# Sixteen blocks of the FFN's input turned through DRAM and VectorE instead of TensorE, with new places for the E x E stage's sums, softmax halves and look-ups

## The chip, the cores and the metric

One core of one Trainium2 chip runs the whole kernel. The metric is the device time of one execution in microseconds (us). All data is fp32. The engines are named as the profile names them: PE is TensorE (PEld its weight loads), DVE is VectorE, ACT is ScalarE, POOL is GpSimd, SP is SyncE, which issues most DMAs.

## The reference, cut to what matters

x has the shape (2, 2048, 512): 4096 tokens, 512 columns. The attention has no square of tokens: its scores are 512 x 512 (columns by columns, "E x E").

```python
n = layernorm(x)                                   # per token
q, k, v = n @ Wq, n @ Wk, n @ Wv
a = softmax((q^T k) / sqrt(16), axis=-1)           # (2, 512, 512): summed over tokens
x = x + (a v^T)^T @ Wo
g, u, d = lut[gate_idx], lut[up_idx], lut[down_idx]   # 16 values; indices 1376 x 512, 512 x 1376
f = layernorm(x)
x = x + (silu(f @ g^T) * (f @ u^T)) @ d^T
```

## The kernel before, in words

**Blocks and chunks.** 128 tokens are a block; there are 32 (NBLK). Four are a chunk c (NCH is 8), two chunks a pair p (NPR is 4). Every product of matrices is done as a seven-product scheme (Winograd's form of Strassen's), so each operand has extra sums (S1 to S4, T1 to T4), which DVE forms.

**Stages in order of time.**
1. *Gram* (lines 355 to 494): ACT normalizes each block (L175), PE adds up n^T n (L363). The normalized blocks are stored to DRAM (`nd`): those of chunks 3 to 7 as they are made (L361), those of chunks 0 to 2 made a second time by `n_stored` (L458), four each beside chunks 3, 4 and 5. After chunk 5, SP issues the loads of wk and wq, 1 MB each (L336).
2. *E x E* (lines 496 to 634 and 738 to 742): the batch's Gram matrix times the weights, four products for each of two batches: p1, s, t1, m. Each is one call of `square`, which issues seven stages: `a1`, `c1`, the `a4` of the square before, `a2`, `b1`, `c2`, `a3`. A stage is eight PE matmuls (L508); its result is copied by ACT (a1, c1, a2, a4) or added by DVE (b1, c2, a3). The a-stages add up in one PSUM bank, so a2 must wait until ACT has copied a1's result, and a3 for a2's. After each stage come the extra instructions that `beside` lists for it, and `pump(0.7)`. The softmax lies between s and t1: `exp(h)` is a row maximum (DVE, L576), a scaling of it (L577) and two exponentials (ACT, L579); `end(h)` is a reciprocal (DVE, L586) and two scalings (ACT, L588). h is a half of the matrix's rows.
3. *y* (lines 743 to 755): for block k PE forms y = n m (L665). n comes back from `nd` turned: four 64 KB loads a block (`n_load`, L650) and one transpose of 32 x 32 squares on DVE (`n_turned`, L656). `side(k, bank)` then works on earlier blocks: `added(k-1)` adds y to x and starts the second norm, `f_normed(k-6)` normalizes (ACT, L175), `f_turned(k-8)` turns block k-8 for the FFN with four PE transposes (L689) and an ACT copy (L692). `f_summed(p)` forms the FFN's four sums for a pair of chunks. Then `pump(1.0)`.
4. *FFN* (lines 1036 to 1057): 11 tiles f of the 1376 inner columns, for each the four pairs p. A unit `GateUp(f, p)` has the stages a1, c1, (the last unit's) a4, a2, c2, b, a3, eight matmuls each (L769), and after each stage a call of `between()`: 7 slots a unit, 6 in the first. A slot takes the next entry of `todo`, or, when that is empty, calls `pump(0.9)`. `todo` begins with nine entries: what `side` still has to do for blocks 24 to 31, and the last two pairs' sums.
5. *Down* (lines 1064 to 1087): the last product, and the output.

**The order of work** is the program's own on PE, ACT, DVE and SP (`manual_schedule`): nothing overtakes on an engine. PE has 8 PSUM banks.

**The look-ups.** DVE turns 4-bit indices into values by bit tests: `looked_up` (L295) walks a list of 17 jobs: gu0, gu1, wd0 to wd3, gu2, gu3, wd4, gu4, gu5, wd5, gu6 to gu10. Job gu f makes the gate and up weights of FFN tile f: 3 mask pieces, 8 selects (L222), 7 merges (COPY_PREDICATED, L234), then 4 sums. Each piece has a cost in the program's own units: masks 0.74, 0.65 and 0.37, a select 0.75, a merge 1.27, a sum 0.42; a gu job 18.3 and a wd job 16.6 in all. `pump(us)` adds `us` to a budget and issues pieces until it is used up. A gu job waits at a gate until tile f-2 is done (L274). Before tile f starts, whatever is left of job gu f is issued at once:

```python
for f in range(NFT):
    while "S4" not in gu[f]:
        next(lookup)
    ...
    for p in range(NPR):
        ...
        line.run(GateUp(f, p))
    passed[0] = f + 1
```

Of the kernel before, what the change touches and what calls it, by code (L numbers as in the profile page):

```python
# [35 lines left out]
F32 = mybir.dt.float32  # L39
# [10 lines left out]
P = 128  # L50
# [6 lines left out]
def tile_attn_ffn(  # L57
# [13 lines left out]
    nc = tc.nc  # L71
# [33 lines left out]
    wd = wdp.tile([P, NFT, E], F32, tag="wd", name="wd")  # L105
    x1d = dram.tile([NCH, P, J, E], F32, tag="x1d", name="x1d")
    nd = dram.tile([NCH, J, P, E], F32, tag="nd", name="nd")
    hd = dram.tile([NCH, NFT, P, CH], F32, tag="hd", name="hd")


# [2 lines left out]
    def room(tag, name):  # L113
        return keep.tile([P, J, E], F32, tag=tag, name=name)
# [13 lines left out]
    class Norm:  # L128
# [41 lines left out]
            stt(rstd, q, 1.5, r0, ALU.add, ALU.mult)  # L170
            stt(nmr, mean, self.minus, rstd, ALU.mult, ALU.mult)

        def normed(self, j, block, xn=None):
            xn = xn or xnp.tile([P, E], F32, tag="xn", name=f"xn_{self.name}_{j}", bufs=4)
            nc.scalar.activation(  # L175
                xn, block, AF.Identity, bias=self.nmr[:, j : j + 1],
                scale=self.rstd[:, j : j + 1],
            )
            return xn
# [132 lines left out]
    def pump(us):  # L312

        owed[0] = min(owed[0] + us, 2 * us + 1.0)
        while owed[0] > 0:
            cost = next(lookup, None)
            if cost is None:
                return
            owed[0] -= cost
# [140 lines left out]
    for c in range(1, NCH):  # L460
        for j in range(J):
            gram(c, j)
            if STORED <= c < STORED + 3:
                n_stored()
            if c + 1 < NCH and j < 2:
                for i in (2 * j, 2 * j + 1):
                    ln1[c + 1].stats(i, xc[c + 1][:, i, :])
                if j == 1:
                    ln1[c + 1].sqrt(0, J)
            elif c + 1 < NCH and j == 2:  # L470
                pump(0.6)
                ln1[c + 1].rest(0, J)
                pump(0.6)
            elif ahead and c > STORED + 2:
                for op in ahead[:4]:
                    op()
                del ahead[:4]
            else:
                pump(1.9)
            if c == 1 and j == 2:  # L480
                nc.vector.tensor_tensor(
                    lut_x, lut_pairs[:, :, 0], lut_pairs[:, :, 1], ALU.bitwise_xor
                )
            if c == CPB and j == 1:
                gram_out(0)
            if c == CPB + 1 and j == 3:
                wk_sb = load_weight(wk, "a0", "wk_sb")
                wq_sb = load_weight(wq, "a1", "wq_sb")
                wk_ops = right(wk_sb, "wk")
                ahead += wk_ops.todo  # L490
            if c == CPB and j == 3:
                gram_mirror(0)
                g_ops = [left(gs[0], "g_0")]
                ahead += g_ops[0].todo
# [52 lines left out]

    before = [None]

    def square(a, b, dest, name, beside):  # L550

        u = Square(a, b, dest, name)
        last, before[0] = before[0], u
        stages = [u.a1, u.c1, last.a4 if last else lambda: None, u.a2, u.b1, u.c2, u.a3]
        for i, stage in enumerate(stages):
            stage()
            for op in beside.get(i, ()):
                op()  # L560
            pump(0.7)

    class Softmax:

# [32 lines left out]
    assert not ahead  # L597
    square(g[0], wk_ops, p1[0], "p1_0", {
        1: [lambda: gram_mirror(1)], 4: g[1].todo[:2], 5: g[1].todo[2:],
    })  # L600
    square(g[1], wk_ops, p1[1], "p1_1", {
        3: wq_ops.todo[:2], 4: wq_ops.todo[2:], 5: p1_ops[0].todo[:2], 6: p1_ops[0].todo[2:],
    })
    wo_sb = load_weight(wo, "a0", "wo_sb")
    wo_ops = right(wo_sb, "wo")
    att = [room(f"sq{b}", f"a_{b}") for b in range(B)]
# [1 line left out]
    att_ops = [left(att[b], f"att_{b}", ("S1", "S2", "S4")) for b in range(B)]  # L608
    square(wq_ops, p1_ops[0], att[0], "s_0", {
        4: p1_ops[1].todo[:2], 5: p1_ops[1].todo[2:], 6: [lambda: soft[0].exp(1)],  # L610
    })
    square(wq_ops, p1_ops[1], att[1], "s_1", {
        0: [lambda: soft[0].end(1)], 2: [lambda: soft[0].exp(0)], 3: [lambda: soft[0].end(0)],
        4: wo_ops.todo[:2], 5: [*wo_ops.todo[2:], *att_ops[0].todo[:1]],
        6: [*att_ops[0].todo[1:], lambda: soft[1].exp(1)],
    })

    wvT_sb = room("a1", "wvT_sb")
    for k in range(KB):
        for i in range(KB):  # L620
# [1 line left out]
                wvT_sb[:, k, :].rearrange("p (m c) -> p m c", m=KB)[:, :, i * Q : (i + 1) * Q],  # L622
                wvT[k * P : (k + 1) * P, i * P : (i + 1) * P].rearrange("p (m a) -> p m a", a=Q),
            )
    wv_ops = left(wvT_sb, "wv", ("S2", "S1", "S4"))
    t1 = [room(f"a{2 + b}", f"t1_{b}") for b in range(B)]
    t1_ops = [right(t1[b], f"t1_{b}", ("T1", "T2", "T4")) for b in range(B)]
    square(att_ops[0], wo_ops, t1[0], "t1_0", {
        0: [lambda: soft[1].end(1)], 2: [lambda: soft[1].exp(0)], 3: [lambda: soft[1].end(0)],
        5: att_ops[1].todo[:2], 6: att_ops[1].todo[2:],  # L630
    })
    square(att_ops[1], wo_ops, t1[1], "t1_1", {
        4: wv_ops.todo[:2], 5: wv_ops.todo[2:], 6: t1_ops[0].todo,
    })


    nls, nTs, ys, xfs = {}, {}, {}, {}
    xb, xs = {}, {}

    def block(k):  # L640
        return xc[k // J][:, k % J, :]

    def n_load(k):

        if k < NBLK:
            c, j = divmod(k, J)
            nls[k] = sums.tile([P, P // Q, P], F32, tag="e", name=f"nl_{k}")
            rows = nd[c, j].rearrange("(t b) e -> b t e", b=Q)
            for i in range(KB):
                nc.sync.dma_start(nls[k][i * Q : (i + 1) * Q], rows[:, :, i * P : (i + 1) * P])  # L650

    def n_turned(k):

        if k < NBLK:
            nTs[k] = sums.tile([P, KB, P], F32, tag="e", name=f"nT_{k}")
            nc.vector.transpose(  # L656
                nTs[k].rearrange("p m (t b) -> p m t b", b=Q),
                nls[k].rearrange("p t (m a) -> p m t a", a=Q),
            )

    def y_product(k):
        ys[k] = bank(f"y_{k}")
# [6 lines left out]
    def added(k):  # L669
# [6 lines left out]
        if j == J - 1:  # L676
            ln2[c].sqrt(0, J)
            nc.sync.dma_start(x1d[c], xc[c])

    def f_normed(k):  # L680
        xfs[k] = ln2[k // J].normed(k % J, block(k))

    def f_turned(k, bank):
        c, j = k // J, k % J
        if j == 0:
            xb[c] = room(f"x{c - 1}" if c else "a0", f"xb_{c}")
        ps = bank(f"xt_{k}")
        for i in range(KB):
            nc.tensor.transpose(  # L689
                ps[:, i * P : (i + 1) * P], xfs[k][:, i * P : (i + 1) * P], ident  # L690
            )
        nc.scalar.copy(  # L692
            xb[c][:, :, j * P : (j + 1) * P], ps.rearrange("p (k t) -> p k t", k=KB)
        )

    def f_summed(p):

        r = {}

        def half(tag, h):  # L700
            if tag not in r:
                r[tag] = halves.get(tag)
                if r[tag] is None:
                    r[tag] = halves[tag] = room(tag, f"xT_{tag}")
            return r[tag][:, 2 * h : 2 * h + 2, :]

        t1, t2, t4 = (half(*at) for at in SUMS_AT[p])
        b11, b21 = xb[2 * p][:, 0:2, :], xb[2 * p][:, 2:4, :]
        b12, b22 = xb[2 * p + 1][:, 0:2, :], xb[2 * p + 1][:, 2:4, :]
        sub(t1, b12, b11)  # L710
        sub(t2, b22, t1)
        sub(b12, b22, b12)
        sub(t4, b21, t2)
        xs[p] = {"11": b11, "21": b21, "22": b22, "T3": b12, "T1": t1, "T2": t2, "T4": t4}

    halves = {}
    SUMS_AT = [
# [3 lines left out]
        [("sq1", 1), (f"x{NCH - 1}", 0), (f"x{NCH - 1}", 1)],  # L721
    ]

    def side(k, bank):

        if 0 <= k - 8 < NBLK:
            f_turned(k - 8, bank)
        if k - 1 < NBLK:
            added(k - 1)
        if k % J == 1 and 0 <= (k - 5) // J < NCH:  # L730
            ln2[(k - 5) // J].rest(0, J)
        if 0 <= k - 6 < NBLK:
            f_normed(k - 6)
        done = (k - 12) // J
        if k % J == 0 and done in (1, 3):
            f_summed(done // 2)

    m_sb = [room(f"sq{b}", f"m_{b}") for b in range(B)]
    square(wv_ops, t1_ops[0], m_sb[0], "m_0", {4: t1_ops[1].todo[:2], 5: t1_ops[1].todo[2:]})
    square(wv_ops, t1_ops[1], m_sb[1], "m_1", {  # L740
# [2 lines left out]
    for k in range(NBLK):  # L743
        if k:
            n_turned(k + 1)
            n_load(k + 3)
        y_product(k)
        if k == 0:
            before[0].a4()
            n_turned(1)  # L750
            n_load(2)
            n_load(3)
        else:
            side(k, bank)
        pump(1.0)
    pps.release()
    sums.release()
    ffn = tc.alloc_tile_pool(name="ffn", bufs=1, reuse_waits="tile")
# [116 lines left out]
        else:  # L875
            pump(0.9)

    def tr(name):
        return psum("tr", name)

    def drained(k):
        side(k, tr)
        if k == NBLK + 1:
            f_summed(2)

    todo += [lambda k=k: drained(k) for k in range(NBLK, NBLK + 8)]
    todo.append(lambda: f_summed(3))


    wd_ops = []  # L890
# [145 lines left out]
# [3 lines that stand above are left out]
        if f == NFT - 1:  # L1039
# [8 lines left out]
            h = Hidden(0)  # L1048
            todo += by_two(down_sums(hps["dT"]))
        for p in range(NPR):  # L1050
            if f == NFT - 1 and p == 1:
                h.rest_of()
                todo += by_two(h.sums())
            if f == NFT - 1 and p == 3:
                units = [Down(h, 0)]
            line.run(GateUp(f, p))
# [82 lines left out]
```

## Time and profile before

| | |
|---|---|
| median of 3 runs | 1118.92 us (1118.81 to 1119.29) |
| the profiled execution | 1118.62 us, span 1116.6 us |
| first matmul, end of the last | 7.1 us, 1112.5 us |
| PE transposes of the FFN's input (L689) | 128, four for each of 32 blocks |
| DVE transposes (L656) | 32, 702 ns each |
| the L175 ACT pass of one block | 803 to 805 ns |
| copy of a turned block (L692) | 586 ns |
| merge (L234), select (L222) | 1304 ns, 804 ns |
| 128x512 add or subtract on DVE | 680 to 692 ns |

Stages by the timeline: Gram's matmuls to 81.6 us, E x E to 185.5, y to 307.3, FFN to 842, Down to 1112.5. The profile's page gives busy shares, the span in 40 slices, the chain of work that ended last, and groups of instructions; "idle before" is the time an engine stood still ahead of an instruction, with what released it. Instructions on DVE and ACT overlap their neighbours a little, so that two in a row start closer together than one lasts.

### The profile page before, as it was taken

How to read it: one execution, taken by the hardware profiler on the slowest of the kernel's cores; microseconds unless marked ns; L12 is line 12 of the kernel's file. 1: busy time of each engine (PE TensorE's matmuls, PEld its weight loads, DVE VectorE, ACT ScalarE, POOL GpSimd, SP SyncE). 2: the span in 40 equal slices, each digit the busy share in tenths (PEclk: the TensorE clock that was granted, in tenths of full speed). 3: DMA queues.
4: the chain of work that ended last, by engine and by line, in shares of the span. 5: the costliest groups of instructions: out<-in, count | busy, mean ns of one | idle time of the engine just before them, and what ended most of it. 6: DMA issues, size and time to landing. Idle time of an engine off the chain costs nothing.

```text
span 1116.6 us, 10381 instructions
## 1 busy us (share of the span) xinstructions
PE 1095.0 (98%) x3580; PEld 659.6 (59%) x3580; DVE 684.1 (61%) x1251; ACT 310.9 (28%) x583; POOL 14.7 (1%) x31
## 2 busy tenths in 40 slices
PE   7999899999999999999999999999999999999998
PEld 4668677444454444444444444444437888888887
DVE  6877887677766757788777575855553344333341
ACT  4642332456562222222322222222221000000000
POOL 0000000000000000000000000000000000000000
PEclk9999999999999999999999999999999999999999
DMA  8460302444211111111111111111415443345421
GB/s 337 173 226 21 74 19 76 157 137 140 94 57 66 56 48 66 57 54 55 68 62 51 57 38 69 40 38 49 144 47 179 156 160 121 107 164 167 159 66 38
DMA packets 72180, 108.76 MB, mean 97 GB/s; under 512 B 15152, under 2 KB 31536, under 8 KB 70208
## 3 DMA queue, kind: packets, MB, share of 16 engines
q1 hardware_dynamic: 69936, 100.70, 26.7%
q0 software_dynamic: 2192, 7.41, 2.2%
q8 instruction: 28, 0.46, 0.2%
q14 instruction: 24, 0.20, 0.1%
HBM read 60.37 MB, written 47.71 MB: 97 GB/s over the span
## 4 chain that ended last, share of the span: by engine, by line
PE 94%; DVE 3%; ACT 1%; DMA 1%; issue 0%; SPq 0%; DVEq 0%; ACTq 0%
PE a_g L769 27%; PE a_d L769 14%; PE c_g L769 14%; PE y L665 10%; PE c_d L769 7%; PE b_g L769 7%; PE gp L363 5%; PE b_d L769 4%; PE xt L689 1%; PE ea_p L508 1%; PE ea_m L508 1%; DMA nd<-xn_a 1%; PE ea_t L508 1%; PE ec_m L508 1%; PE ec_p L508 1%; ACT a L579 0%
## 5 line engine op out<-in xcount | busy, mean ns | idle before, releaser
L125 DVE TENSOR_TENSOR c<-c_g,u 128x512 f32<-128x512 f32 (+1 forms) x44 | 30.4, 690 | 146.2 <-PE c_g L769 139.4
L665 PE MATMUL y<-m,nT 128*128 128x512 f32 x256 | 114.0, 592 | 0.0
L769 PE MATMUL c_g<-xb,w 128*128 128x512 f32 (+1 forms) x176 | 82.8, 593 | 0.8 <-DVE w L122 0.8
L769 PE MATMUL a_g<-xb,s 128*128 128x512 f32 (+1 forms) x176 | 82.8, 592 | 0.8 <-DVE c L125 0.8
L769 PE MATMUL a_g<-xb,w 128*128 128x512 f32 (+1 forms) x176 | 82.7, 592 | 0.0
L769 PE MATMUL b_g<-xb,w 128*128 128x512 f32 (+1 forms) x176 | 82.7, 592 | 0.0
L769 PE MATMUL a_g<-xT_a,s 128*128 128x512 f32 (+1 forms) x176 | 82.7, 592 | 0.0
L363 PE MATMUL gp<-xn_a 128*128 128x512 f32 (+3 forms) x256 | 72.4, 445 | 8.7 <-ACT xn_a L175 8.7
L665 PEld LDWEIGHTS y<-m,nT 128*128 128x128 f32 x256 | 46.8, 190 | 49.4 <-issue 49.0
L821 ACT ACTIVATE h<-h 128x512 f32<-128x512 f32 (+1 forms) x44 | 27.7, 630 | 161.9 <-DVE h L125 161.9
L363 PEld LDWEIGHTS gp<-xn_a 128*128 128x128 f32 x256 | 45.1, 196 | 35.8 <-issue 16.6
L769 PE MATMUL a_g<-xT_sq,s 128*128 128x512 f32 (+1 forms) x132 | 62.0, 592 | 0.0
L222 DVE TENSOR_SCALAR gu<-idx_gu,lut_x,lut_sb 128x1024 int32<-128x1024 int32 (+1 forms) x77 | 59.1, 792 | 0.0
L769 PEld LDWEIGHTS a_g<-xb,s 128*128 128x128 f32 (+1 forms) x176 | 32.8, 188 | 43.2 <-issue 38.9
L769 PEld LDWEIGHTS c_g<-xb,w 128*128 128x128 f32 (+1 forms) x176 | 32.8, 188 | 42.7 <-issue 41.1
L769 PEld LDWEIGHTS b_g<-xb,w 128*128 128x128 f32 (+1 forms) x176 | 32.9, 188 | 42.0 <-issue 42.0
L769 PEld LDWEIGHTS a_g<-xT_a,s 128*128 128x128 f32 (+1 forms) x176 | 32.9, 188 | 41.5 <-issue 41.5
L769 PEld LDWEIGHTS a_g<-xb,w 128*128 128x128 f32 (+1 forms) x176 | 32.9, 188 | 41.5 <-issue 41.3
L234 DVE COPY_PREDICATED gu<-b_gu,gu 128x1024 f32<-128x1024 int16 (+1 forms) x44 | 56.2, 1278 | 0.7
L769 PE MATMUL a_d<-dT,hs_a 128*128 128x256 f32 x224 | 56.2, 379 | 0.0
L234 DVE COPY_PREDICATED wd<-b_wd,wd 128x1024 f32<-128x1024 int16 (+1 forms) x42 | 50.9, 1213 | 0.5
L125 DVE TENSOR_TENSOR r<-r,a_d 128x256 f32<-128x256 f32 x32 | 13.5, 421 | 54.8 <-PE a_d L769 54.8
(238 smaller groups left out, 1736.6 us busy)
## 6 DMA issues: line engine op xcount, KB each, us to landing
hd<-h SPq DMA_DIRECT2D x80, 256.0 KB, 2.0
h<-hd SPq DMA_DIRECT2D x40, 512.0 KB, 6.7
nl<-nd SPq DMA_DIRECT2D x128, 64.0 KB, 2.0
x1d<-x SPq DMA_DIRECT2D x8, 1024.0 KB, 4.3
r<-x1d SPq DMA_DIRECT2D x32, 256.0 KB, 4.0
out_dram<-r SPq DMA_DIRECT2D x32, 256.0 KB, 2.4
x<-in_x_dram SPq DMA_DIRECT2D x7, 1024.0 KB, 14.1
nd<-xn_a SPq DMA_DIRECT2D x20, 256.0 KB, 2.1
```

Source lines behind the costliest of these rows:

```text
L125: nc.vector.tensor_tensor(dest, a, b, ALU.add)
L222: vec.tensor_scalar(dest.bitcast(I32), idx, lut_x[:rows, k : k + 1], lut_i[:rows, at : at + 1], ALU.bitwise_and, ALU.bitwise_xor,)
L234: vec.copy_predicated(dest, masks[level - 1], t)
L363: nc.tensor.matmul(gp[b][i][:, i * P :], xn[:, i * P : (i + 1) * P], xn[:, i * P :], start=c % CPB == 0 and j == 0, stop=c % CPB == CPB - ...
L508: nc.tensor.matmul(ps[:, m, :], self.a[a][:, k, m * P : (m + 1) * P], self.b[b][:, k, :], start=first and m == k == 0, stop=k == 1, skip_g ...
L665: nc.tensor.matmul(ys[k], nTs[k][:, i, :], m[:, i, :], start=(i == 0), stop=(i == KB - 1))
L689: nc.tensor.transpose(ps[:, i * P : (i + 1) * P], xfs[k][:, i * P : (i + 1) * P], ident)
L769: nc.tensor.matmul(ps, lhsT, rhs, start=first and i == 0, stop=i == len(pairs) - 1, skip_group_check=not first,)
L821: nc.scalar.activation(self.h0, self.h0, AF.Silu)
```

## The change

**Turning.** Blocks 16 to 31 (`EARLY` is 16) are no longer turned by PE. ACT writes their normalized rows with the columns in another order (`quarters`), SP stores them to a new DRAM tensor `xnd`, four 64 KB loads bring each back (`f_load`), and one DVE transpose (`f_turned_late`) puts it in its place. Store and load are 5 blocks apart in the y stage, load and transpose 2. What remains after y is 20 entries of `todo` instead of 9. The FFN's sums become a generator with one sum a step: pairs 0 and 1 over four blocks of y each, pairs 2 and 3 over entries of `todo`.

**E x E.** `square` takes a list of seven pump rates; the softmax halves and the sums of wo, att, wv and t1 are listed at other stages. In y, `pump` gets 1.0 up to block 21 and 0.5 after that.

**Gram.** `n_stored` runs beside chunks 3, 5 and 6 instead of 3, 4 and 5.

```diff
-            if STORED <= c < STORED + 3:
+            if c in (CPB - 1, CPB + 1, CPB + 2):
                 n_stored()
...
-            pump(0.7)
+            pump(rate[i])
...
     square(g[0], wk_ops, p1[0], "p1_0", {
...
-    })
+    }, (1.2, 1.2, 1.2, 1.2, 0.3, 0.3, 1.2))
     square(g[1], wk_ops, p1[1], "p1_1", {
...
-    })
+    }, (1.2, 1.2, 1.2, 0.3, 0.3, 0.3, 0.3))
...
     square(wq_ops, p1_ops[0], att[0], "s_0", {
         4: p1_ops[1].todo[:2], 5: p1_ops[1].todo[2:], 6: [lambda: soft[0].exp(1)],
-    })
+    }, (1.0, 1.0, 1.0, 1.0, 0.3, 0.3, 0.3))
     square(wq_ops, p1_ops[1], att[1], "s_1", {
-        0: [lambda: soft[0].end(1)], 2: [lambda: soft[0].exp(0)], 3: [lambda: soft[0].end(0)],
-        4: wo_ops.todo[:2], 5: [*wo_ops.todo[2:], *att_ops[0].todo[:1]],
-        6: [*att_ops[0].todo[1:], lambda: soft[1].exp(1)],
-    })
+        1: [lambda: soft[0].end(1)], 2: [lambda: soft[0].exp(0)], 3: wo_ops.todo[:2],
+        4: [lambda: soft[0].end(0)], 5: [*wo_ops.todo[2:], *att_ops[0].todo[:2]],
+        6: att_ops[0].todo[2:],
+    }, (0.5, 0.5, 0, 0, 0, 0, 0))
...
     square(att_ops[0], wo_ops, t1[0], "t1_0", {
-        0: [lambda: soft[1].end(1)], 2: [lambda: soft[1].exp(0)], 3: [lambda: soft[1].end(0)],
-        5: att_ops[1].todo[:2], 6: att_ops[1].todo[2:],
-    })
+        1: [lambda: soft[1].exp(1)], 2: [lambda: soft[1].exp(0)], 3: [lambda: soft[1].end(1)],
+        4: [lambda: soft[1].end(0)], 5: att_ops[1].todo[:2], 6: att_ops[1].todo[2:],
+    }, (0, 0, 0.5, 0.5, 0.5, 0, 0))
     square(att_ops[1], wo_ops, t1[1], "t1_1", {
-        4: wv_ops.todo[:2], 5: wv_ops.todo[2:], 6: t1_ops[0].todo,
-    })
+        2: wv_ops.todo[:1], 3: wv_ops.todo[1:2], 4: [*wv_ops.todo[2:3], t1_ops[0].todo[0]],
+        5: [*wv_ops.todo[3:], t1_ops[0].todo[1]], 6: t1_ops[0].todo[2:],
+    }, (1.0, 1.0, 0.7, 0.7, 0, 0, 0))
...
+    EARLY = NBLK // 2
+
     def f_normed(k):
-        xfs[k] = ln2[k // J].normed(k % J, block(k))
+        c, j = divmod(k, J)
+        xfs[k] = ln2[c].normed(j, block(k), quarters=k >= EARLY)
+        if k >= EARLY:
+            nc.sync.dma_start(xnd[c, j], xfs[k])
...
+    def f_load(k):
+        fls[k] = xnp.tile([P, E], F32, tag="xn", name=f"fl_{k}", bufs=4)
+        reload(fls[k], xnd[k // J, k % J])
+
+    def f_turned_late(k):
+        turn(f_place(k), fls[k])
...
-        if 0 <= k - 8 < NBLK:
-            f_turned(k - 8, bank)
+        if 0 <= k - 8 < EARLY:
+            f_turned(k - 8)
...
+        if k - 11 in range(EARLY, NBLK) and k < NBLK:
+            f_load(k - 11)
+        if k - 13 in range(EARLY, NBLK) and k < NBLK:
+            f_turned_late(k - 13)
+        p, i = divmod(k - 16, 2 * J)
+        if 0 <= p < NPR // 2 and i < 4:
+            if i == 0:
+                f_pairs[p] = f_sums(p)
+            next(f_pairs[p])
...
-        pump(1.0)
+        pump(1.0 if k < EARLY + 6 else 0.5)
...
-    todo += [lambda k=k: drained(k) for k in range(NBLK, NBLK + 8)]
-    todo.append(lambda: f_summed(3))
+    for i, what in enumerate([
+        dict(turns=[19], loads=[21]), dict(turns=[20], loads=[22]), dict(loads=[23]),
+        dict(turns=[21]), dict(turns=[22], loads=[24]), dict(turns=[23], loads=[25]),
+        dict(pair=2), dict(pair=2, turns=[24], loads=[26]), dict(pair=2),
+        dict(turns=[25], loads=[27]), dict(pair=2, turns=[26], loads=[28]),
+        dict(turns=[27], loads=[29]), dict(turns=[28], loads=[30]), dict(turns=[29], loads=[31]),
+        dict(turns=[30]), dict(turns=[31]), dict(pair=3), dict(pair=3), dict(pair=3), dict(pair=3),
+    ]):
+        late(i, **what)
```

`late` appends one entry to `todo`: the first eight call `side` as before, then come the listed transposes, loads and one sum of the pair.

## The prediction

> **What bounds the kernel now.** I read the page first. PE is busy for 98% of the span and in every slice:
>
> ```profile
> PE 1095.0 (98%) x3580; PEld 659.6 (59%) x3580; DVE 684.1 (61%) x1251; ACT 310.9 (28%) x583; POOL 14.7 (1%) x31
> ```
>
> The chain of waits gives PE 94%. So the time is PE's work plus PE's waits. An edit counts when it takes work from PE, ends a PE wait, or makes a new one. Second, PE's own waits:
>
> ```profile
> PE gp L363 <- ACT xn_a L175: 8.7, 3, 7.1
> PE ea_t L508 <- ACT t L520: 2.8, 1, 2.8
> PE ec_t L508 <- DVE a L122: 1.6, 1, 1.6
> PE ec_m L508 <- DVE t L122: 1.3, 1, 1.3
> PE c_g L769 <- DVE w L122: 0.8, 1, 0.8
> ...
> PE ea_s L508 <- ACT a L520: 0.4, 1, 0.4
> PE ea_s L508 <- ACT a L529: 0.3, 1, 0.3
> PE ea_t L508 <- ACT t L529: 0.3, 1, 0.3
> ```
>
> Of the 8.7, 7.1 is the start. Six lines lie in E x E; one (`c_g <- w`) is a look-up that came late. Third, the chain by time, for what PE's transposes cost:
>
> ```profile
> 218.24 0.44 PE xt L689 x4
> 218.68 3.43 PE y L665 x8
> 222.12 0.44 PE xt L689 x4
> ```
>
> Four transposes take 0.436 us of PE between two y products of 3.43.
>
> **Transposes off PE.** 16 blocks x 0.436 = **-7.0**, eight blocks in y, eight in the FFN. That is all PE gets back if nothing new makes it wait. What replaces them:
> - DVE, 16 transposes of 0.70. In y (k 29 to 31) a period falls to 3.43; DVE has n_turned 0.62, added 0.70, pump about 0.5, the transpose 0.62, every fourth block 0.96 of norm: 2.4 to 3.4. For k 24 to 27 a sum of 1.15 stands in its place: 3.0, or 3.9 once, under a block (3.43) of lead. Hidden.
> - ACT, 16 copies of 586 ns fewer. The re-ordered write of L175 is not in the trace. Nearest rows: L692's copy into pieces and a plain copy both 586 ns; a DVE transpose 702 against 680 for an add. So 0 to 3% of 803 ns; I take 0. Doubled it would still fit a period in which ACT works 1.8.
> - SP, 16 stores (0.32 to issue, landing in 2.1) and 64 loads (0.43, landing in 2.0). A load stands two blocks (6.9) before its transpose in y. Hidden there.
>
> **E x E.** From the timeline, start to start, a stage takes 1.727. The six late ones lose 0.59, 0.44, 1.76, 2.98, 0.44, 1.44, and each restart 0.1 more: 8.25. The costliest, with its columns start, duration, engine, line, instruction:
>
> ```profile
> 138.08 0.72 ACT L579 ACTIVATE a<-a,nb 128x512 f32<-128x512 f32 x1 [8.61 <-DVE nb L577]
> ...
> 139.50 0.56 ACT L520 COPY t<-ea_t 128x512 f32<-128x512 f32 x1
> ```
>
> The copy that t1_0's a2 needs is queued on ACT behind exponentials that waited for a row maximum. I walked the new order through with these rows' durations (add 0.60, after its own operand 0.72; maximum 1.25; scaling of it 0.2; exponential pair 1.43, scaling pair 1.24, copy 0.56; time stamps as before up to 115):
> - s_0: two look-up sums leave the place ahead of a3's add, which starts at 117.67, not 118.34. Exponentials at 119.84; a1's copy, now ahead of `end(1)`, is done at 121.83, and a2 is due at 121.96: 0.1 left of 0.59.
> - s_1: maximum 124.04, exponentials 125.50, a2's copy done 127.50; a3 is due at 127.25: 0.3 and a restart of 0.1 remain. This wait isn't removed.
> - wo's first sums go ahead of `end(0)`; att's S3 is ready at 130.03, needed at 131.1: 1.76 gone.
> - t1_0: `exp(1)` stands behind c1's copy, so a1's copy (131.9) is early for a2 (134.56): 2.98 gone. Next late is a2's copy behind `exp(0)`: 139.41 against 139.74. It fits by 0.3.
> - t1_1's a1 (141.47) needs `end(0)`, done at 141.90: 0.3 new.
> - t1's T3 is formed at 152.1, needed at 155.3: 1.44 gone.
>
> Left: 0.8 of 8.25, so **-7.4**. Bounds: -5.5 (t1_0's a2 copy and one more miss by a maximum each) and -8.2.
>
> **Gram.** Four L175 passes and stores move from chunk 4 to 6, behind the 2 MB of weights in SP's queue. Chunk 7's passes need the stores of chunk 6, which landed at 71.80, 72.42, 73.05, 73.67; with a store between each pair the spacing is 1.25, and 1.11 is PE's per block: **+0.4** (0 to 1).
>
> **The look-ups: the new wait.** Count the budget in the program's units; it can be counted without a time. Gram's pumps are unchanged and issue 22.9. E x E before: 56 x 0.7 = 39.2; now 32.0. y before: 32; now 22 x 1.0 + 10 x 0.5 = 27. So the FFN starts at 94 before, at 82 now. The slots without pump grow from 9 to 20. Tile 2 starts at slot 55 (6 + 7 x 7). Before, wd3 is done at slot 19, the gate opens at 27, gu2 is done at slot 45, ten ahead. Now 35 slots x 0.9 bring 82.1 to 113.6, but gu2 ends at 3 x 18.3 + 4 x 16.65 = 121.6. In whole pieces what is left is a merge, two selects, three merges and the four sums. The `while` ahead of tile 2 issues them in one go, and PE's next matmul needs the last merge. The trace shows this place once, at tile 4, where two sums were left:
>
> ```profile
> 499.69 1.30 DVE L234 COPY_PREDICATED w<-b_gu,gu 128x1024 f32<-128x1024 int16 x1
> 500.89 0.67 DVE L125 TENSOR_TENSOR h<-b_g,p 128x512 f32<-128x512 f32 x1
> 501.85 0.69 DVE L125 TENSOR_TENSOR c<-a_g,p 128x512 f32<-128x512 f32 x1 [0.29 <-PE a_g L769]
> 502.46 0.68 DVE L827 TENSOR_TENSOR h<-h,c 128x512 f32<-128x512 f32 x1
> 503.06 0.42 DVE L125 TENSOR_TENSOR s<-w 128x256 f32<-128x256 f32 x1
> ```
>
> PE started tile 4 at 501.65. Laid on this pattern, tile 2 has DVE busy with: merge to 500.89, add, select 501.50, add 502.22, product 502.83, select 503.43, then the burst from 504.27: merge 1.21, selects 0.72 and 0.83, merges 1.34, 1.34 (each needs the one before) and 1.31, done at 511.02. That is 9.4 after PE's due start, with the restart **+9.5** (8.5 to 10.5). Nothing covers it: PE is in order and its bank is free.
>
> At tile 4 the same count leaves the last merge for the slot before and all four sums for the burst: merge 500.95, add 502.16, product 502.77, last merge 503.37 to 504.68, so PE waits 3.1 where it waited 0.95: **+2.1** (1.5 to 2.6).
>
> **The clock after 9 us of idling.** The trace has PE starting cold: the first 128x512 matmuls took 1141 ns, later ones 594:
>
> ```profile
> L363 PE MATMUL gp<-xn_a 128*128 128x512 f32 x2 | 2.1, 1141 | 7.1 <-ACT xn_a L175 7.1
> ...
> L363 PE MATMUL gp<-xn_a 128*128 128x512 f32 x25 | 12.9, 594 | 0.0
> ```
>
> (the first line for the window from 7, the second for 13 to 40). The first block lasted 4.43 (7.10 to 11.53), the second 2.49, the third 2.16: the start cost 2.27 + 0.33 = 2.6. Idling of 2.8 at 137 was followed by matmuls of full speed; at the end the granted clock is 1.00 until 1114.7 and then 0.50, 2.2 after the last matmul. Nine us of idling is beyond both, so I take **+2.6** (0, as after 137, to 3.4). The Trainium skill, "TensorE: Matmul & The Clock Gate", Part 1, speaks against the change here: by it an idle window of about 3.4 us halves the clock and as long a busy one restores it, which would be an estimated 1.7 in place of 2.6 and the total 0.9 lower; the start in this trace, 5 us to full speed, is longer than the page's window.
>
> **FFN's first 20 slots.** A slot is now 1.72 instead of 2.15 for the first eight. ACT: a1's copy, the last block's statistics and one L175 pass stand ahead of c1's copy, done 5.2 after the FFN's start; c2 is due at 5.15: +0.2. DVE: 13 transposes (8.1), 8 sums (9.2), 1.7 of norm, and 2.9 units' own work at 3.1 make 28 in 34.3. But SP's loads wait in turn for the 1 MB x1d store, for L175 and for DVE's products, and landings push DVE some 3 us late at slots 4 to 12. Pair 3's third sum is then done at 36.5 and c1 of that unit due at 36.05. **+0.5** together (0 to 1.5).
>
> **Sum.** -7.0 - 7.4 + 0.4 + 9.5 + 2.1 + 2.6 + 0.5 = +0.7 on the profiled execution's 1118.62, which lies 0.3 below the median of the three runs: **1119.3**. No change that a measurement of this kernel can tell, which is about 0.2%, or 2.2 us.
>
> **Rivals.**
> - *The clock stays* and the small terms are nothing: -7.0 - 8.2 + 9.5 + 2.1 = -3.6, so 1115. For it: 2.8 us of idling cost nothing. Against it: the half clock at the end came sooner. 0.15.
> - *The look-ups aren't late*, since the budget runs differently from my count: without 9.5, 2.1 and 2.6 the time would be 1105. Against it: the count puts the job starts of before where the trace has their first mask (gu2 358.9, gu3 406.9, gu4 469.0). 0.02.
> - *Slower: the second trip through DRAM holds DVE* in slots 9 to 20, where a load is followed by its transpose two slots (3.4 us) later. From about 4.5 us per load on, the lateness reaches PE at pair 3. y's loads took up to 8 us (262.06 to 270.04) behind an x1d store, which is what stands ahead here too. Price 3 to 5: 1123. Against it: the median is 2.0. 0.17.
> - *The clock also falls at tile 4*: the idling there is some 2.8, as at 137 where it did not; 2.6 more, 1121.9. 0.08.
>
> The forecast's own case has the remaining 0.58, 1116.8 to 1121.2. Range 1115.3 to 1123.3, which cuts off the tail of the first and third rivals and the second. Faster 0.17, same 0.58, slower 0.25 (the third and fourth rivals).
>
> **What would show it.** PE's waits: one of about 9.4 for a merge (`w`, L234) at the start of tile 2, one of about 3 at tile 4; in E x E one of about 0.3 at s_1's a3, nothing over 1. Matmuls at 514 or so above 1.1 us for some 5 us. y periods of 3.43 from block 24 on. L689 with 64 transposes. I'd be wrong if the burst is shorter, if E x E keeps a wait of over 1 us, or if PE waits in slots 0 to 20 by more than 1.5.

## The result, and the profile after

| | before | after |
|---|---|---|
| median, lowest, highest (us) | 1118.95, 1118.10, 1119.39 (6 runs) | 1124.19, 1121.76, 1127.84 (6 runs) |
| ratio of the times | 1 | 1.0050, 95% interval 1.0031 to 1.0069 |
| profiled execution, its span | 1118.62, 1116.6 | 1127.84, 1125.7 |
| mean granted clock of PE | 0.999 | 0.991 |

The change made the kernel slower by 0.5%, 0.9 us beyond the range's upper end. "No change" was forecast. The profiled execution of after is the slowest of its six. Its parts below add up to +9.2 where the medians differ by +5.2; where those 4 us lie is told under "The step under both", further down.

The code moved down by some lines: the merges are L242 (L234 before), the adds L128 and L125, the turning transposes L661, the FFN's matmuls L808, E x E's L516, the remaining PE transposes L712. The loads of `xnd` are issued at L657, its stores at L701. An FFN stage is four PE instructions in the trace, not eight as written above; a stage of E x E is eight. (One 128x512 product of the program shows there as two PE instructions.)

The page's busy times and its row of the granted clock, after:

```profile
PE 1095.9 (97%) x3516; PEld 656.0 (58%) x3516; DVE 696.3 (62%) x1267; ACT 303.6 (27%) x567; POOL 14.6 (1%) x31
...
PEclk9999999999999989998999999999999999999999
```

PE has 64 instructions fewer, yet it was busy 0.9 longer: some matmuls ran slowly. The clock row shows two slices below 9, the 15th and the 19th (394 to 422 and 507 to 535). PE's own waits, after (sum, times, longest):

```profile
PE a_g L808 <- DVE w L242: 11.8, 2, 9.2
...
PE c_g L808 <- DVE xb L125: 2.3, 1, 2.3
PE a_g L808 <- DVE c L128: 2.1, 2, 1.4
...
PE ea_s L516 <- ACT a L537: 0.3, 1, 0.3
```

Of the six E x E waits of before one of 0.3 is left. Two waits for a merge came (9.2 at tile 2, 2.7 at tile 4), and two more in the FFN's tile 0: 1.4 for an add on DVE (`c`, L128) and 2.3 for one of pair 3's sums (`xb`, L125). The first matmuls of each place tell the rest. PE's timeline, after, with the columns start, duration, what, and idle time before; at full speed a stage starts 1.72 after the one before:

```profile
337.36 3.68 PE L808 MATMUL c_g<-xb,w 128*128 128x512 f32 x4 [2.33 <-DVE xb L125]
340.84 1.92 PE L808 MATMUL a_g<-xb,s 128*128 128x512 f32 x4
...
406.88 3.78 PE L808 MATMUL a_g<-xb,w 128*128 128x512 f32 x4 [9.19 <-DVE w L242]
410.46 2.94 PE L808 MATMUL c_g<-xb,w 128*128 128x512 f32 x4
413.24 1.88 PE L808 MATMUL a_g<-xb,s 128*128 128x512 f32 x4
...
508.76 3.78 PE L808 MATMUL a_g<-xb,w 128*128 128x512 f32 x4 [2.66 <-DVE w L242]
512.33 3.20 PE L808 MATMUL c_g<-xb,w 128*128 128x512 f32 x4
```

After each of the three waits a stage takes about twice its time. It isn't the operands: the same stages elsewhere take 1.72. It is the clock. The windows of after (window, length, busy time of PE, PEld, DVE, ACT, POOL, granted clock, DMA share, GB/s):

```profile
337.50:340.90 3.40, 3.40 (x5) 1.33 (x6) 3.37 (x5) 0.00 (x0) 0.23 (x1) 0.50 0.21 77
402.30:412.60 10.30, 5.72 (x7) 2.52 (x8) 10.09 (x15) 0.59 (x1) 0.71 (x1) 0.50 0.17 51
508.20:515.00 6.80, 6.24 (x8) 2.63 (x9) 6.38 (x12) 0.59 (x1) 0.00 (x0) 0.50 0.10 39
```

The clock was half in all three. Three falls of the clock, then, where the prediction counted on one.

**The account**, in starts of the same instructions, after less before, both profiled executions:

| stretch | measured | forecast |
|---|---|---|
| Gram and E x E, to the first y product | -7.55 | -7.0 (-7.4 + 0.4) |
| y | -3.51 | -3.5 |
| FFN tile 0, without its eight blocks' transposes (-3.49) | +6.56 | +0.5 |
| tile 2's first matmul against tile 1's start (the burst) | +9.36 | +9.5 |
| the rest of tile 2 (the clock) | +2.92 | +2.6 |
| tile 4's wait (2.66 in place of 0.80) and restart | +2.82 less 0.95 | +2.1 |
| the rest of tile 4 (the clock) | +3.1 | 0 |
| sum, transposes of the FFN (-3.49) with it | +9.2 | +0.7 |

So two rows failed: tile 0, and the clock in tile 4. Of tile 0's 6.56, 1.76 is the half clock behind pair 3's wait (that stage took 3.48 from start to start, not 1.72); the rest is waits and their restarts.

### The profile page after: what moved, and what is told of

Read it like the earlier page. It is cut to its first block, busy times and chain, and to the rows that moved or that the text cites. A ratio compares the mean times of both kernels' runs of the same rounds, so it can differ in the third digit from the quotient of the medians.

```text
span 1125.7 us, 10379 instructions
## 1 busy us (share of the span) xinstructions
PE 1095.9 (97%) x3516; PEld 656.0 (58%) x3516; DVE 696.3 (62%) x1267; ACT 303.6 (27%) x567; POOL 14.6 (1%) x31
## 4 chain that ended last, share of the span: by engine, by line
PE 93%; DVE 3%; SPq 1%; ACT 1%; DMA 1%; issue 1%; DVEq 0%; ACTq 0%
PE a_g L808 25%; PE a_d L808 14%; PE c_g L808 13%; PE y L680 10%; PE c_d L808 7%; PE gp L371 6%; PE b_g L808 6%; PE b_d L808 4%; PE ea_t L516 1%; SPq L657 1%; PE ea_p L516 1%; PE ea_m L516 1%; PE ea_s L516 1%; PE xt L712 1%; PE ec_t L516 1%
## 5 line engine op out<-in xcount | busy, mean ns | idle before, releaser
L128 DVE TENSOR_TENSOR c<-c_g,u 128x512 f32<-128x512 f32 (+1 forms) x44 | 30.3, 689 | 145.0 <-PE c_g L808 138.1
L808 PE MATMUL a_g<-xb,w 128*128 128x512 f32 (+1 forms) x176 | 86.5, 615 | 11.8 <-DVE w L242 11.8
L808 PE MATMUL c_g<-xb,w 128*128 128x512 f32 (+1 forms) x176 | 87.0, 619 | 2.3 <-DVE xb L125 2.3
L808 PE MATMUL a_g<-xb,s 128*128 128x512 f32 (+1 forms) x176 | 82.9, 593 | 2.1 <-DVE c L128 2.1
L808 PE MATMUL a_g<-xT_a,s 128*128 128x512 f32 (+1 forms) x176 | 82.8, 593 | 0.1
L808 PE MATMUL b_g<-xb,w 128*128 128x512 f32 (+1 forms) x176 | 82.7, 592 | 0.0
L808 PEld LDWEIGHTS a_g<-xb,w 128*128 128x128 f32 (+1 forms) x176 | 33.8, 194 | 56.2 <-issue 42.7
L808 PEld LDWEIGHTS c_g<-xb,w 128*128 128x128 f32 (+1 forms) x176 | 34.4, 196 | 48.3 <-issue 43.3
L808 PE MATMUL a_g<-xT_sq,s 128*128 128x512 f32 (+1 forms) x132 | 62.0, 592 | 0.0
L808 PEld LDWEIGHTS a_g<-xb,s 128*128 128x128 f32 (+1 forms) x176 | 33.1, 189 | 46.3 <-issue 39.0
L808 PEld LDWEIGHTS a_g<-xT_a,s 128*128 128x128 f32 (+1 forms) x176 | 32.9, 188 | 43.0 <-issue 42.0
L808 PEld LDWEIGHTS b_g<-xb,w 128*128 128x128 f32 (+1 forms) x176 | 33.0, 188 | 42.5 <-issue 42.5
L242 DVE COPY_PREDICATED gu<-b_gu,gu 128x1024 f32<-128x1024 int16 (+1 forms) x44 | 56.4, 1281 | 0.9
L808 PE MATMUL a_d<-dT,hs_a 128*128 128x256 f32 x224 | 56.2, 378 | 0.0
L242 DVE COPY_PREDICATED wd<-b_wd,wd 128x1024 f32<-128x1024 int16 (+1 forms) x42 | 50.9, 1212 | 0.8
L837 ACT COPY p<-a_g 128x512 f32<-128x512 f32 (+1 forms) x44 | 25.7, 584 | 86.0 <-PE a_g L808 86.0
```

The lines of the kernel that those rows point to most:

```text
L128: nc.vector.tensor_tensor(dest, a, b, ALU.add)
L242: vec.copy_predicated(dest, masks[level - 1], t)
L808: nc.tensor.matmul(ps, lhsT, rhs, start=first and i == 0, stop=i == len(pairs) - 1, skip_group_check=not first,)
L837: nc.scalar.copy(self.p1, self.a)
```

## The experiments

Theory A, formed from this account: the burst at tile 2 with its cold restart costs some 12, tile 4 up to 5, SP's issuing of the loads 4 to 5; the E x E edits and the transposes gain what was forecast. Rival theories are in the expectations.

### The look-ups on time

```diff
-            pump(0.9)
+            pump(1.2 if passed[0] < 2 else 1.0 if passed[0] < 4 else 0.9)
```

in `between()`, everything else as after: the budget of tiles 0 to 3 runs faster, so that nothing is left for a burst.

> The changed kernel with larger look-up budgets in the first four FFN tiles (1.2 a slot in tiles 0 and 1, 1.0 in tiles 2 and 3, instead of 0.9), so that by the count no piece is left over at any tile's start. Theory A (the loss is look-ups issued in a burst that PE waits for, and the half clock after it): the wait of 9.2 at tile 2 and of 2.7 at tile 4 disappear from PE's waits, and so do the slow matmuls behind them: 1124.2 - 9.4 - 2.9 - 2.8 - about 1.5 = 1107.6. Rival B (VectorE has no room for these pieces, so they only move the waiting into tiles 0 and 1): PE waits of 5 us or more in all inside tiles 0 and 1, 1118 or above.

Measured: **1107.40** (1106.81 to 1108.54, four runs; before beside it 1118.69), ratio 0.9902 (0.9887 to 0.9916). Theory A's number. The longest of PE's waits behind the start:

```profile
PE c_g L808 <- DVE xb L125: 2.4, 1, 2.4
```

Both waits for merges are gone and none took their place; pair 3's of 2.4 stays, with the slow stage behind it. Against after's +5.2, this is 16.5 us less. Some 1.1 of it is a gain over before: its own late look-up at tile 4 (0.8 and a restart) is on time too. The look-ups that the change displaced out of E x E and y, and what followed from them, are even so more than the whole loss.

### The loads of xnd over two queues

```diff
-    def reload(t, rows):
+    def reload(t, rows, queues=(nc.sync, nc.sync)):
...
-            nc.sync.dma_start(t[i * Q : (i + 1) * Q], rows[:, :, i * P : (i + 1) * P])
+            queues[i % 2].dma_start(t[i * Q : (i + 1) * Q], rows[:, :, i * P : (i + 1) * P])
...
-        reload(fls[k], xnd[k // J, k % J])
+        reload(fls[k], xnd[k // J, k % J], (nc.sync, nc.scalar))
```

> The changed kernel with every second f_load DMA issued by ACT instead of SP. Theory A (pair 3's sums come late because SP needs 1.9 us to issue a block's four loads and works without a pause from 300 to 329): the waits of 1.4 at 322 and 2.3 at 334 go, and the half clock behind the second: 1124.2 - 4.4 - 0.8 = 1119. Rival C (VectorE itself is too full in the first 20 slots): the waits stay, 1124. If ACT's own waits for a free buffer hold up its copies, PE waits for ACT there instead.

Measured: **1119.16** (1116.77 to 1121.56, ten runs), ratio 1.0006 (0.9996 to 1.0016): 4.8 below after's +5.2. Here is why the loads mattered, first SP's own timeline in after (start, busy time, what):

```profile
313.65 7.31 SPq L657 DMA_DIRECT2D fl<-xnd  x12
321.06 0.38 SPq L831 DMA_DIRECT2D hd<-h  x1
321.48 3.77 SPq L657 DMA_DIRECT2D fl<-xnd  x8
```

SP issued so, one behind the other with hardly a pause, from 301.5 to 329.5, as a rule 0.47 from one load to the next, four loads to a block (one issue, at 316.1, took 1.99, for a reason that the trace doesn't show): it was itself the bound, and the loads left it late, one block every 2 us or more. Their landing was not slow: 2.3 from issue, as in the group of DMA issues. DVE paid first: in after it stood 1.20, 1.87 and 1.08 for loads ahead of the last three transposes (326.9 to 331.3), and pair 3's sums come behind these. Its waits for the loads in after, then in this run:

```profile
DVE xb L661 <- DMA fl<-xnd: 14.9, 12, 2.5
```

```profile
DVE xb L661 <- DMA fl<-xnd: 7.2, 6, 2.8
```

and PE last. PE's timeline of this run at the place where after has 2.33 of waiting and a slow stage:

```profile
333.49 1.98 PE L808 MATMUL c_g<-xb,w 128*128 128x512 f32 x4 [0.40 <-DVE xb L125]
```

0.40, and a stage of full speed behind it. Pair 3's third sum was done 37.0 after the FFN's start, where the forecast had 36.5 and after 40.8. The wait of 1.4 at 323 went too, so DVE had room for its own work in these slots. The burst of 9.2 at tile 2 stayed, as it should: the two losses are separate. After tile 4's wait, 2.66 here too, the stage lasted 1.98: this time the clock stayed.

### The idle time filled

After, with nine matmuls of an identity, whose result nothing reads, ahead of tile 2's first product:

```diff
+            if f == 2 and p == 0:
+                idle = fps.tile([P, E], F32, tag="idle", name="idle", bufs=1)
+                for _ in range(9):
+                    nc.tensor.matmul(idle, ident, xs[0]["11"][:, 0, :], start=True, stop=True)
...
             line.run(GateUp(f, p))
```

> The changed kernel with nine 128x512 matmuls on PE ahead of tile 2, into a PSUM bank that nobody reads, which fill 7.7 of the 9.2 us in which PE waits there. Theory A (idling lowers the clock, and the first 5 to 6 us after it run at half speed): the wait shown shrinks to about 1.5, the matmuls behind it last 592 ns, the time falls by 2.9 to 1121.3. Rival D (the half clock is no result of the idling, or costs nothing): 1124 or more.

Measured: **1121.42** (1119.58 to 1123.00, ten runs), ratio 1.0025 (1.0016 to 1.0035): 2.5 below after's +5.2, with useless work added. PE's timeline (the nine products are 18 PE instructions):

```profile
396.94 7.89 PE L1112 MATMUL idle<-xb,ident 128*128 128x512 f32 x18
406.33 1.98 PE L808 MATMUL a_g<-xb,w 128*128 128x512 f32 x4 [1.50 <-DVE w L242]
```

The burst still ends at 406.3, so its 9 us are still lost, but tile 2 begins at full speed. That separates the burst (9.4) from the clock (2.9 in the trace, 2.5 here in medians).

### The E x E order alone, and the turning alone

One kernel is before with nothing but after's E x E section: the lists of `beside`, the seven rates of each `square`, and the order of wv's sums. The other is the version of the next section, but with before's E x E section put back.

> The kernel before with the E x E stage's new order and pump rates alone; turning, Gram, y and FFN as before. By the count its look-ups are as much in time as before (three pieces left at tile 4). Theory A: E x E is 7.6 shorter and nothing is given back: 1118.95 - 7.6 = 1111.4. Rival E (the smaller budgets of the squares are paid later by waits for look-ups): 1116 or above.

Measured: **1111.23** (1110.70 to 1111.43, four runs), ratio 0.9934 (0.9919 to 0.9949): -7.5, where -7.4 was forecast. Two of PE's waits (L508 and L770 are this kernel's lines of the E x E and FFN matmuls); the second is all that E x E has left:

```profile
PE c_g L770 <- DVE w L122: 0.8, 1, 0.8
...
PE ea_s L508 <- ACT a L529: 0.3, 1, 0.3
```

By the count E x E's lower rates delay the look-ups here too, but y's `pump(1.0)` and the nine entries of `todo` were left as they were, and tile 4's old wait of 0.8 didn't grow: the cut in E x E alone makes no look-up late.

> The same with the E x E stage of the kernel before (its order and its 0.7 rates): turning and Gram's moved stores, with both repairs. Theory A: the turning is worth 7.0 less the waits that stay in tile 0 (1.0), and 1.0 at tile 4: 1118.7 - 7.0 = 1111.7, so that the two gains add up to that of both within 0.5. Rival G (the turning's gain is partly taken back by VectorE in the y stage, hidden in the other runs): y periods above 3.43 from block 24 on, 1114 or more.

Measured: **1112.33** (1111.22 to 1112.80, four runs; before beside it 1119.23), ratio 0.9937 (0.9920 to 0.9954): -6.9. The transposes give back what PE spent on them, if nothing new is late. That the sum is so near 7.0 is partly chance: it holds the 1.1 at tile 4, which the faster budget gives, and losses of about the same size. One of these stands in its timeline; first the same place in before, then here:

```profile
140.12 1.99 PE L508 MATMUL ea_t<-T_wo,S_att 128*128 128x256 f32 x8 [2.82 <-ACT t L520]
```

```profile
140.09 3.45 PE L516 MATMUL ea_t<-T_wo,S_att 128*128 128x256 f32 x8 [2.82 <-ACT t L528]
```

This is the wait of 2.8 at 137 that the prediction took as proof that such idling is free. In the profile of before the stage behind it lasted 1.99. Here, behind the same wait of the same instruction, it lasted 3.45. That cost 1.4, of which 0.9 was left where y began.

### Both new waits gone

After, with the edits of the first two experiments together.

> The changed kernel with both repairs: larger look-up budgets in tiles 0 to 3 and every second f_load issued by ACT. Theory A: what is left is the gains, E x E 7.6 and turning 7.0, the 1.0 that tile 4 waited before, less about 1.0 of waits in tile 0: 1118.7 - 14.6 = 1104, with no half clock between start and end. Rival F (the two repairs disturb each other, since tile 1's fuller VectorE and ACT's queue meet): 1106 or more with a new wait above 1 us in tile 0 or 1.

Measured: **1104.12** (1103.39 to 1104.46, four runs; before beside it 1119.23), ratio 0.9866 (0.9852 to 0.9881): 15.1 below before and some 20 below after; the fastest version here. The page's busy times:

```profile
PE 1087.8 (99%) x3516; PEld 653.5 (59%) x3516; DVE 695.1 (63%) x1267; ACT 303.9 (28%) x567; POOL 14.7 (1%) x31
```

PE is busy 8.1 less than in after with the same 3516 instructions. In after's three windows PE was busy for 15.4 at half clock, which at full speed would have been 7.7: nearly all of it. No wait behind the start's is longer than 0.8, pair 3's is 0.2, and the granted clock's row holds 9 in every slice. The parts add up: -7.5 (E x E alone) and -6.9 (turning alone) make -14.4 for -15.1, and the 0.7 between them is of the size of the 0.9 that the slow stage just shown cost, in the turning-alone kernel only. The tile 4 gain of 1.1 is in both -6.9 and -15.1.

### Idling in doses

What decides whether the clock falls? Two kernels, each the version just shown, with a stated number n of in-place multiplications by 1.0 on DVE, which change no value, ahead of seven FFN tiles, so that PE idles there for 1.9 to 5.9 us:

```diff
+            if p == 0:
+                for _ in range({3: 2, 4: 3, 5: 4, 6: 5, 7: 6, 8: 8, 9: 12}.get(f, 0)):
+                    nc.vector.tensor_scalar_mul(gu[f]["11"], gu[f]["11"], 1.0)
...
             line.run(GateUp(f, p))
```

(the other kernel has the numbers 6, 5, 12, 4, 3, 2, 8).

> Both repairs, and at the start of tiles 3 to 9 VectorE multiplies a quarter of the tile's weights by one 2, 3, 4, 5, 6, 8 and 12 times, which holds PE up for idle times of about 2.0, 2.5, 2.9, 3.4, 3.8, 4.7 and 6.5 us. It asks from which idle time the granted clock falls. If a full window of the clock record (its low stretches are multiples of 3.41) has to be idle, it falls never below 3.4, always above 6.8, by chance between. If less suffices, as at 2.3 and 2.7 in the changed kernel, it falls at some of the doses below 3.4 too. Cost of a fall: 1.7 to 3.4.

> As the doses before, in another order (6, 5, 12, 4, 3, 2 and 8 times at tiles 3 to 9): the same idle times meet other moments of the record. If the fall is set by the idle time alone, the same doses fall in both; if by where in a window the idling lies, doses between about 2 and 5 differ from run to run.

One execution each: 1142.83 and 1140.33, of which 24.4 are the seven added waits. What counts is the 14 idle stretches:

| idle (us) | 1.91 | 2.24 | 2.24 | 2.57 | 2.90 | 2.90 | 3.23 | 3.25 | 3.70 | 3.88 twice, 5.00, 5.19, 5.88 |
|---|---|---|---|---|---|---|---|---|---|---|
| clock fell | no | yes | no | yes | yes | no | yes | no | yes | yes |

No threshold of length fits: 2.24 fell and 3.25 didn't. The same wait of 2.24, PE's timeline of the first kernel and then of the second:

```profile
495.97 3.68 PE L808 MATMUL a_g<-xb,w 128*128 128x512 f32 x4 [2.24 <-DVE w L1111]
```

```profile
659.42 1.98 PE L808 MATMUL a_g<-xb,w 128*128 128x512 f32 x4 [2.24 <-DVE w L1111]
```

What fits is the phase. In every trace here the granted clock changes only at instants that lie a multiple of 3.413 us apart. Windows of the first kernel laid on that grid, columns as before; an idle of 2.24 ends at 495.97, one of 3.25 at 549.25:

```profile
492.69:496.10 3.41, 1.17 (x4) 0.32 (x3) 2.32 (x7) 0.63 (x1) 0.00 (x0) 1.00 0.22 84
496.10:499.52 3.42, 3.42 (x5) 1.35 (x6) 3.38 (x7) 0.00 (x0) 0.00 (x0) 0.50 0.14 55
...
547.29:550.70 3.41, 1.45 (x4) 0.73 (x5) 3.31 (x10) 0.00 (x0) 0.00 (x0) 1.00 0.57 216
550.70:554.10 3.40, 3.40 (x10) 1.49 (x9) 2.17 (x4) 1.17 (x2) 0.00 (x0) 1.00 0.00 0
```

The 2.24 lay inside one window: PE worked 1.17 of it, was idle for 66%, and the next window ran at 0.50. The 3.25 was cut by an edge: PE worked 1.45 of the fuller one, was idle for 57%, and the clock stayed. Over all traces here the clock fell each time that one window was idle for over 58%, never at 53% or less, and at 57 to 58% it went both ways. 58% of 3.413 is 2.0 us. So by this reading one stretch of idling below 2.0 us doesn't bring the clock down, one above 4.0 always does, since it fills some window that far wherever the edge lies, and between them it is a matter of the edge.

A fixed length of idling, whichever, is thereby refuted. That the window is what the chip counts in is read from these coincidences; nothing here could move the window itself.

## Why the prediction was wrong, point by point

- **Transposes off PE, -7.0: right.** -3.51 in y, and -3.49 for eight blocks in the FFN, where stages now start 1.72 apart instead of 2.15. In the timeline of after y's last eight blocks are one run of 64 products without a gap, 27.6 long, which is 3.45 a block, and 64 transposes are left at L712.

  The re-ordered ACT write was rightly taken at about 0: the 16 re-ordered passes took 804 ns on average, the 16 plain ones of the same run 799.
- **E x E, -7.4: right**, -7.5. The walk left 0.8 of waiting; 0.28 was there (s_1's a3). t1_1's a1, forecast 0.3 late, was in time.
- **Gram, +0.4: nothing.** Too small to matter, and in its range.
- **The burst at tile 2, +9.5: right**, +9.36, of the length and in the order that the budget's count gave. DVE's timeline, after, from the second piece of the burst on:

```profile
401.31 1.53 DVE L230 TENSOR_SCALAR gu<-idx_gu,lut_x,lut_sb 128x1024 int32<-128x1024 int32 x2
402.87 2.62 DVE L242 COPY_PREDICATED gu<-b_gu,gu 128x1024 f32<-128x1024 int16 x2
405.53 1.30 DVE L242 COPY_PREDICATED w<-b_gu,gu 128x1024 f32<-128x1024 int16 x1
```

  A merge, two selects, three merges, and PE started at 406.88, when the last was done. The count of the program's own pacing budget needs no trace, and with DVE's times from tile 4 it held to 0.2 us.
- **The clock after 9 us, +2.6: right**, +2.9, and by the experiment that filled the idle time 2.5. The closeness is in part luck: behind the same wait of 9.2 in the run with two queues the rest of tile 2 lost 1.9.
- **The FFN's first 20 slots, +0.5: this step failed.** It came to +6.6 in the profiled execution. By the medians the second queue gave back 4.8, nearly the whole 4.9 between the forecast 1119.3 and the measured 1124.19. The text saw that the loads "wait in turn", and took DVE some 3 us late until slot 12, with 36.5 after the FFN's start for pair 3's third sum. It was done at 40.8. What was not summed was SP's own time in these slots: mostly 0.47 a load with four loads a block, and stores between, where PE's slot had shrunk to 1.72. This is the third rival, at its place and its price (3 to 5), to which the text gave 0.17. But its switch, a landing of 4.5 us a load, wasn't what happened: loads landed in 2.3 and were issued late.
- **Tile 4, +2.1: the wait right, the step incomplete.** The wait grew by 1.9. The clock fell behind it, 3.1 more in the profiled execution: the fourth rival, given 0.08. In the traces of the second queue and of the filled idle time the same wait (2.66 and 2.67) was followed by a stage of 1.98, so this part is there in some executions and not in others.
- **The step under both: "idling of 2.8 at 137 was followed by matmuls of full speed".** One observation was made a rule. By the doses, 2.3, 2.7 and 2.8 are all in the range where the phase decides, so at pair 3 and at tile 4 a fall of 1.7 to 3.1 us was, by estimate, about an even chance, and stood in the sum at nothing. This is also where most of after's spread comes from, 6.1 us over six runs against 1.1 over four of the quickest version. The mean granted clock of after's runs goes from 0.991 in the slowest to 0.995 in the fastest; times the span, that is 10.1 and 5.6 us of lost clock, 4.5 of the 6.1. And 10.1 is the half of 20.5, the sum of the three windows at 0.50 shown above. Only the slowest run has a trace, so in which places the other five were spared is not shown.

The Trainium skill, "TensorE: Matmul & The Clock Gate", Part 1, which the prediction set against the start's row, has a free-running window of 3413 ns, and the changes of the clock in these traces agree with it. Its rule that an idle window, or gaps of over about 3.4 us, brings the clock down is too narrow for them: all gaps of 3.70 and more did, but so did one of 2.24.

Of the two sides, then, the gains (-14.4 apart, -15.1 together) were sized to within 1, the burst and its restart to within 0.4 each, and the loss that the sum lacked came from two places that were named as rivals and held for unlikely, both at once.

## What to carry to other kernels

Work that is moved off a saturated engine is a gain only if what is displaced is still on time: here an edit worth some 14 us lost 0.5%. A pacing budget was cut in two stages and 11 more slots went without it, nobody raised it behind them, and one line in `between()` returned 16.5 us; the rest was an issuing engine that nobody had summed. When loads are added, sum the issuing engine's time over the slots they fall in, not only the time to landing. A wait of the bounding engine costs its length and, from some 2 us on, may cost a restart at half clock as well; one trace without it proves nothing.

## What the runs showed of the hardware

- The clock's grid of 3.413 us and the share of about 58% of one window, from 14 doses and the waits of the other traces. A fall cost 1.4 to 1.8 us where the clock was half for one window (3.41), and 1.9 to 3.1 where it was for two or three (idle parts counted in).
- Nine useless matmuls, which kept PE at work for 7.7 of 9.2 us, kept the clock and saved 2.5 us.
- An issue of a 64 KB load took SP mostly 0.43 us, 0.47 with the step to the next. A block's four loads are 1.9, about as long as one load's landing (2.1 to 2.3), so a second issuing queue was worth 4.8 us of kernel time.
